# Cross-attention on one core: queries and outputs as seven block products in place of eight

## The chip, the cores and the metric

The kernel runs on one core of a Trainium2 chip. The metric is the device time of one execution in microseconds, as the median of several runs. In the profile PE is TensorE, PEld its loading of weights, DVE is VectorE, ACT is ScalarE, POOL is GpSimd, and SP is the engine whose queue issues most DMAs. All data are fp32.

## The reference, cut to what matters

Four layers of cross-attention, each followed by a feed-forward part, are added to x (4 batch elements of 256 tokens, 256 wide). The context has 4 x 512 rows of 128. Layers 1, 2 and 3 have the same attention, and the change is in them:

```python
def _L1_xattn_ref(text_hidden, vision_tokens, vision_mask, Wq, Wk, Wv, Wo):
    # N_HEADS = 16, N_KV_HEADS = 8, HEAD_DIM = 128, D_TEXT = 256, D_VISION = 128
    q = (text_hidden @ Wq).reshape(B, T_text, N_HEADS, HEAD_DIM).transpose(0, 2, 1, 3)
    k = (vision_tokens @ Wk).reshape(B, T_vis, N_KV_HEADS, HEAD_DIM).transpose(0, 2, 1, 3)
    v = (vision_tokens @ Wv).reshape(B, T_vis, N_KV_HEADS, HEAD_DIM).transpose(0, 2, 1, 3)
    k = jnp.repeat(k, GROUPS, axis=1)
    v = jnp.repeat(v, GROUPS, axis=1)
    scores = jnp.einsum('bhtd,bhsd->bhts', q, k) / scale
    ...
    attn = jax.nn.softmax(scores, axis=-1)
    out = jnp.einsum('bhts,bhsd->bhtd', attn, v)
    return out.transpose(0, 2, 1, 3).reshape(B, T_text, N_HEADS * HEAD_DIM) @ Wo
...
x = x + _L1_xattn_ref(_layernorm(x, axis=-1), ctx_1024, mask_BxS2_bf1, L1_xattn_Wq, L1_xattn_Wk, L1_xattn_Wv, L1_xattn_Wo)
x = x + _L1_ffn_ref(_layernorm(x, axis=-1), ...)
```

The feed-forward part of layer 1 routes each token to 2 of 8 experts, that of layer 2 picks one of two networks per token, and that of layer 3 works on 64 chosen tokens of each batch element.

## The kernel before

The weights are folded ahead of each of the three attention stages: `m_sb` holds Wq times Wk per head (256 x 128), `n_sb` holds Wv times Wo per head (128 x 256). With them a head's queries are 128 wide, its scores are products with the context itself (`cT`), its values are the context (`c_sb`), and its output is a product with `n_sb`.

`attention(L, ...)` runs over 32 units in order: 4 batch elements `b`, and in each of them 8 pairs of heads `hp`. One unit does, as the code is written:

- `queries` of the next unit (L1689): 4 matmuls of 256 columns into a PSUM bank `mm`, copied to `qT` by ACT (L1697).
- `heads`: 4 score matmuls of 512 columns (L1704) into banks `s`, an exponential of each on ACT (L1707), 4 value matmuls (L1710) into a bank `o`, a copy to `oT` (L1714). POOL adds two halves of the 4 exponentials (`half`, L1717).
- `summed`: DVE adds again (L1723), turns 32x32 blocks (L1725) and reduces (L1729), which gives the sums for the softmax.
- Every fourth unit, `quotients`: a matmul `pz` (L1734), on DVE a bound and a reciprocal `rz` (L1743, L1744), and for each of 4 pairs a transpose `wide` on DVE (L1747) and a product on POOL (L1751) that divides `oT`.
- At `hp == 3`, `output` of the batch element before: for both halves of its tokens, 16 matmuls of 256 columns (L1760) into a bank `mm`, added to `x_sb` by DVE (L1768).

`wide` and `turned` share a ring of two buffers, as do the two buffers of each PSUM bank name. Between the units stand the layernorm of the next batch element (statistics, tokens, transposes) and, through `after`, steps of the feed-forward part for the batch element before; in layer 3 these are the router's.

The engines PE, ACT, DVE and POOL work in program order here:

```python
with tc.manual_schedule(engines={E.PE, E.Activation, E.DVE, E.Pool}):
    attention(1, *mn, after=beside1)
```

So an instruction that waits holds back all that its engine has queued behind it. The end of a stage, after the last unit, reads:

```python
output(B - 1, 0, 0, H // 2)
quotients(B - 1, 1, last=True)
if at_end:
    at_end()
output(B - 1, 1, 0, H // 2)
for c in range(NC):
    output(B - 1, c, H // 2)
```

With `last=True` two of the four products of the quotients are on DVE. The weights of the feed-forward parts (`wgu`, `wd1`, `wd2`, `wds` in layer 1) are loaded into a pool `fwp` during attention, by SP's queue.

Of the kernel before, what the change touches and what calls it, by code (L numbers as in the profile page):

```python
# [9 lines left out]
F32 = mybir.dt.float32  # L10
# [3 lines left out]
ALU = mybir.AluOpType  # L14
# [3 lines left out]
P = 128  # L18
B, S, D = 4, 256, 256
# [816 lines left out]
def bounded_path(ctx: ExitStack, tc: tile.TileContext, t, out: bass.AP, over):  # L836
# [815 lines left out]
    fwp = ctx.enter_context(tc.tile_pool(name="fwp", bufs=1))  # L1652
# [21 lines left out]
    def attention(L, m_sb, n_sb, first_xnT=None, after=None, at_end=None):  # L1674
# [4 lines left out]

        with tc.tile_pool(name=f"att{L}", bufs=2) as ap:  # L1680
            xnTs, xns, norms, qTs, outs, sums = {}, {}, {}, {}, {}, {}
            units = [(b, hp) for b in range(B) for hp in range(H // 2)]

            def queries(b, hp):
                u = f"{L}_{b}_{hp}"
                pq = bank("mm", [P, 2, S], f"pq{u}")
                for j in range(2):
                    for d in range(ND):
                        nc.tensor.matmul(  # L1689
                            pq[:, j, :],  # L1690
                            lhsT=m_sb[:, d, 2 * hp + j, :],
                            rhs=xnTs[b][:, d, :],
                            start=(d == 0),
                            stop=(d == ND - 1),
                        )
                qTs[b, hp] = ap.tile([P, 2 * S], F32, tag="qT", name=f"qT{u}")
                nc.scalar.copy(qTs[b, hp], pq.rearrange("p j s -> p (j s)"))  # L1697

            def heads(b, hp):
                u = f"{L}_{b}_{hp}"  # L1700
                pT = ap.tile([P, NK, 2 * S], F32, tag="pT", name=f"pT{u}")
                for k in range(NK):
                    ps = bank("s", [P, 2 * S], f"ps{u}_{k}")
                    nc.tensor.matmul(  # L1704
                        ps, lhsT=cT[:, b, k * P : (k + 1) * P], rhs=qTs[b, hp], start=True, stop=True
                    )
                    nc.scalar.activation(pT[:, k, :], ps, AF.Exp, bias=mbias[:, b, k : k + 1])  # L1707
                po = bank("o", [P, 2 * S], f"po{u}")
                for k in range(NK):
                    nc.tensor.matmul(  # L1710
                        po, lhsT=c_sb[:, b, k, :], rhs=pT[:, k], start=(k == 0), stop=(k == NK - 1)
                    )
                raw = ap.tile([P, 2 * S], F32, tag="oT", name=f"oT{u}", bufs=H // 2 + 5)
                nc.scalar.copy(raw, po)  # L1714
                outs.setdefault(b, []).append(raw)
                half = ap.tile([P, 2, 2 * S], F32, tag="half", name=f"half{u}", bufs=1 if L == 1 else 2)
                nc.gpsimd.tensor_tensor(half, pT[:, 0:2], pT[:, 2:4], ALU.add)  # L1717
                return half
# [12 lines left out]
            def quotients(b, quarter, last=False):  # L1731
                u = f"{L}_{b}_{quarter}"
                pz = bank("t", [P, 4, NB], f"pz{u}")
                nc.tensor.matmul(  # L1734
                    pz.rearrange("p i f -> p (i f)"),
                    lhsT=quad,
                    rhs=sums.pop((b, quarter)).rearrange("p i f -> p (i f)"),
                    start=True,
                    stop=True,
                )  # L1740

                rz = ap.tile([P, 4, NB], F32, tag="rz", name=f"rz{u}")
                nc.vector.tensor_scalar(rz, pz, 1.0e-37, None, ALU.max)  # L1743
                nc.vector.reciprocal(rz, rz)  # L1744
                for i in range(4):
                    wide = ap.tile([P, NB, 32], F32, tag="turned", name=f"wide{u}_{i}")
                    nc.vector.transpose(wide, rz[:, i, :, None].to_broadcast([P, NB, 32]))  # L1747
                    oT = outs[b][4 * quarter + i]

                    eng = nc.vector if last and i % 2 else nc.gpsimd  # L1750
                    eng.tensor_tensor(oT, oT, wide.rearrange("p f i -> p (f i)"), ALU.mult)  # L1751

            pys = {}

            def output(b, c, h0=0, h1=H):
                if h0 == 0:
                    pys[c] = bank("mm", [P, D], f"py{L}_{b}_{c}")
                for h in range(h0, h1):
                    t0 = (h % 2) * S + c * P
                    nc.tensor.matmul(  # L1760
                        pys[c],
                        lhsT=outs[b][h // 2][:, t0 : t0 + P],
                        rhs=n_sb[:, h, :],
                        start=(h == 0),
                        stop=(h == H - 1),
                    )
                if h1 == H:
                    nc.vector.tensor_tensor(x_sb[b][:, c, :], x_sb[b][:, c, :], pys[c], ALU.add)  # L1768

            xnTs[0] = first_xnT if first_xnT is not None else layernorm(0, f"a{L}_0")[1]  # L1770
            queries(*units[0])
            for n, (b, hp) in enumerate(units):
                if b + 1 < B:
                    if hp == 2:
                        norms[b + 1] = Norm(b + 1, f"a{L}_{b + 1}")
                    elif hp == 4:
                        xns[b + 1] = norms[b + 1].tokens()
                    elif hp == 6:
                        xnTs[b + 1] = layernorm_T(xns[b + 1], f"a{L}_{b + 1}")
                if n + 1 < len(units):  # L1780
                    queries(*units[n + 1])
                half = heads(b, hp)
                if hp == 1 and b > 0:
                    quotients(b - 1, 1)
                if hp == 5:
                    quotients(b, 0)
                summed(b, hp, half)
                if hp == 3 and b > 0:
                    for c in range(NC):
                        output(b - 1, c)  # L1790
                if after:
                    after(b, hp)
            output(B - 1, 0, 0, H // 2)
            quotients(B - 1, 1, last=True)
            if at_end:
                at_end()
            output(B - 1, 1, 0, H // 2)
            for c in range(NC):
                output(B - 1, c, H // 2)
# [7 lines left out]
    FL = FE - P  # L1807
    with tc.issue_after(done["raw"]):
# [7 lines left out]
        )  # L1816
        wd1 = load_fw(
            "fb",
            [P, NE, D],
            lambda w: [(w, t["F1_wdT"][:FR, :].rearrange("(e f) n -> f e n", f=FE)[:P])],  # L1820
            "wd1",
        )
        wd2 = load_fw(
            "fc",
            [P, NE, D],
            lambda w: [(w[:FL], t["F1_wdT"][:FR, :].rearrange("(e f) n -> f e n", f=FE)[P:])],
            "wd2",
# [10 lines left out]
            "wds",  # L1838
        )
# [12 lines left out]
    f1s = ExitStack()  # L1852
    fx = f1s.enter_context(tc.tile_pool(name="f1x", bufs=1))
# [101 lines left out]
    with tc.manual_schedule(engines={E.PE, E.Activation, E.DVE, E.Pool}):  # L1955
# [4 lines left out]
        ):  # L1960

# [286 lines left out]

    with tc.issue_after(done["raw"]):
# [433 lines left out]
```

## Time and profile before

| | |
|---|---|
| median of 3 runs | 1534.7 us (1533.01 to 1537.58) |
| profiled execution | 1532.39 us, its span 1530.6 us |
| granted TensorE clock, mean | 0.988 |
| attention of layers 1, 2 and 3 | about 254 to 596, 731 to 1069 and 1146 to 1499 us of the span |
| PE busy in these three stages | 339.2 of 342.2, 335.5 of 338.5, 344.7 of 352.9 us |
| POOL busy in these three stages | 119.3, 119.4 and 119.3 us |

A row of groups has line, engine, operation, output and inputs with their shapes, the number of instructions, then the busy time in us and the mean ns of one, then the engine's idle time just before them and what ended most of it. A matmul of the code is two PE instructions. Matmuls overlap, so the mean duration of one is longer than the time from one start to the next. A row of a timeline has the start in us from the span's start, the duration, engine, line and operation; neighbouring instructions of one kind are merged.

### The profile page before, as it was taken

The numbers are of one execution on the slowest core, as the hardware profiler recorded it, in microseconds if no ns is written. First come the engines' busy times: TensorE is split into PE (matmuls) and PEld (weight loads), VectorE is DVE, ScalarE is ACT, GpSimd is POOL, SyncE is SP. The second block draws the span as 40 slices with busy tenths as digits, with TensorE's granted clock in tenths as the row PEclk, the third lists the DMA queues.
The fourth block names the chain that finished last, engine by engine and source line by source line (L and its number), as shares of the span: only waits on it lengthen the run. The fifth ranks groups of instructions, "written<-read, shape, count | busy, mean of one in ns | idle before, by whom it ended". The sixth has DMA issues, their size and how long they took to land.

```text
span 1530.6 us, 16401 instructions
## 1 busy us (share of the span) xinstructions
PE 1481.0 (97%) x6243; PEld 935.2 (61%) x6243; DVE 644.9 (42%) x1357; ACT 589.1 (38%) x1047; POOL 474.8 (31%) x354
## 2 busy tenths in 40 slices
PE   8999998999999999999999999999999999999997
PEld 7665676556565567656455656566885565565656
DVE  5666863233534435424233332425442334324363
ACT  4666332442434433234444342422234433423221
POOL 2222343243434331324244342423002343423330
PEclk9999999999999999999999999999999999999999
DMA  4000223100000003135000000000410000000000
GB/s 159 1 1 2 69 69 126 16 0 0 7 1 7 0 3 115 56 86 163 7 0 1 0 1 0 1 0 3 140 55 1 0 1 0 0 1 1 0 0 31
DMA packets 39955, 43.15 MB, mean 28 GB/s; under 512 B 3833, under 2 KB 36826, under 8 KB 39868
## 3 DMA queue, kind: packets, MB, share of 16 engines
q1 hardware_dynamic: 36892, 35.85, 7.4%
q0 software_dynamic: 1872, 5.11, 1.2%
q8 instruction: 52, 0.85, 0.2%
q10 hardware_dynamic: 1104, 1.05, 0.2%
q14 instruction: 35, 0.29, 0.1%
HBM read 36.89 MB, written 5.11 MB: 27 GB/s over the span
## 4 chain that ended last, share of the span: by engine, by line
PE 84%; DVE 9%; POOL 3%; issue 2%; ACT 1%; DMA 0%; POOLq 0%; DVEq 0%; ACTq 0%
PE ps L1704 20%; PE po L1710 20%; PE pq L1689 10%; PE py L1760 10%; PE ph L2308 2%; PE po L2345 2%; PE pgu L2130 2%; PE ps L1313 2%; PE po L1323 2%; PE pyf L1440 1%; POOL oT L1751 1%; PE pyr L2155 1%; PE paf L1390 1%; DVE wide L1747 1%; POOL yg L2169 1%
## 5 line engine op out<-in xcount | busy, mean ns | idle before, releaser
L1717 POOL TENSOR_TENSOR half<-pT 128x1024 f32<-128x1024 f32 x96 | 225.0, 2344 | 579.1 <-ACT pT L1707 406.9
L1704 PE MATMUL ps<-qT,cT 128*128 128x512 f32 x768 | 350.1, 599 | 3.8 <-ACT qT L1697 3.8
L1710 PE MATMUL po<-pT,c_sb 128*128 128x512 f32 x768 | 345.3, 592 | 0.0
L1707 ACT ACTIVATE pT<-ps,mbias 128x512 f32<-128x512 f32 x384 | 263.3, 687 | 77.9 <-PE ps L1704 68.0
L1710 PEld LDWEIGHTS po<-pT,c_sb 128*128 128x128 f32 x768 | 146.0, 190 | 183.6 <-issue 183.1
L1704 PEld LDWEIGHTS ps<-qT,cT 128*128 128x128 f32 x768 | 147.7, 193 | 149.7 <-issue 140.6
L1723 DVE TENSOR_TENSOR half<-half 128x512 f32<-128x512 f32 x96 | 75.0, 782 | 357.4 <-POOL half L1717 357.4
L1689 PE MATMUL pq<-xnT_a,m_sb 128*128 128x256 f32 x768 | 183.4, 383 | 0.7 <-ACT xnT_a L923 0.7
L1760 PE MATMUL py<-n_sb,oT 128*128 128x256 f32 x768 | 169.3, 380 | 1.3 <-POOL oT L1751 1.3
L1689 PEld LDWEIGHTS pq<-xnT_a,m_sb 128*128 128x128 f32 x768 | 143.6, 191 | 39.8 <-issue 14.1
L1760 PEld LDWEIGHTS py<-n_sb,oT 128*128 128x128 f32 x768 | 145.4, 190 | 26.1 <-issue 4.8
L1714 ACT COPY oT<-po 128x512 f32<-128x512 f32 x96 | 56.2, 585 | 263.4 <-PE po L1710 263.4
L1697 ACT COPY qT<-pq 128x512 f32<-128x512 f32 x96 | 56.1, 585 | 255.5 <-PE pq L1689 246.5
L1751 POOL TENSOR_TENSOR oT<-oT,wide 128x512 f32<-128x512 f32 x90 | 121.0, 1375 | 67.3 <-DVE wide L1747 67.3
L1317 ACT ACTIVATE pT<-ps 128x512 f32<-128x512 f32 x128 | 66.1, 603 | 40.8 <-PE ps L1313 40.6
L1747 DVE STREAM_TRANSPOSE wide<-rz 128x512 f32<-128x512 f32 x96 | 65.1, 699 | 28.8 <-POOL oT L1751 28.0
L1725 DVE STREAM_TRANSPOSE turned<-half 128x512 f32<-128x512 f32 x96 | 68.3, 711 | 4.8
L1729 DVE TENSOR_REDUCE sums<-turned 128x16 f32<-128x512 f32 x96 | 65.8, 686 | 3.3
L1743 DVE TENSOR_SCALAR rz<-pz 128x64 f32<-128x64 f32 x24 | 5.4, 224 | 137.1 <-PE pz L1734 137.1
L1768 DVE TENSOR_TENSOR x_sb<-x_sb,py 128x256 f32<-128x256 f32 x24 | 10.1, 421 | 115.9 <-PE py L1760 115.9
L2110 POOL DMA_INDIRECT xg<-xd,who x23 | 22.0, 956 | 59.3 <-PE pxg L2118 33.0
L1313 PE MATMUL ps<-qT,kT 16*128 16x256 f32 x512 | 38.6, 408 | 0.0
(343 smaller groups left out, 1511.3 us busy)
## 6 DMA issues: line engine op xcount, KB each, us to landing
wo<-in_L_wo SPq DMA_DIRECT2D x13, 512.0 KB, 7.1
wq<-in_L_wqT SPq DMA_DIRECT2D x12, 512.0 KB, 4.1
yd<-yr SPq DMA_DIRECT2D x23, 128.0 KB, 1.7
w<-in_F_w SPq DMA_DIRECT2D x2, 1024.0 KB
wgu<-in_F_wgT SPq DMA_DIRECT2D x1, 1760.0 KB, 6.9
wgu<-in_F_wuT SPq DMA_DIRECT2D x1, 1760.0 KB, 10.8
wk<-in_L_wkT SPq DMA_DIRECT2D x12, 128.0 KB, 4.2
wv<-in_L_wvT SPq DMA_DIRECT2D x12, 128.0 KB, 5.9
```

The costliest lines, as they stand in the source:

```text
L1313: nc.tensor.matmul(ps[j][:, k, :], lhsT=kTs[b][r, hg, k0 : k0 + P], rhs=qTs[b][r, hg, :], start=True, stop=True)
L1317: nc.scalar.activation(pT[kp][:, j], ps[j], AF.Exp)
L1689: nc.tensor.matmul(pq[:, j, :], lhsT=m_sb[:, d, 2 * hp + j, :], rhs=xnTs[b][:, d, :], start=(d == 0), stop=(d == ND - 1),)
L1704: nc.tensor.matmul(ps, lhsT=cT[:, b, k * P : (k + 1) * P], rhs=qTs[b, hp], start=True, stop=True)
L1707: nc.scalar.activation(pT[:, k, :], ps, AF.Exp, bias=mbias[:, b, k : k + 1])
L1710: nc.tensor.matmul(po, lhsT=c_sb[:, b, k, :], rhs=pT[:, k], start=(k == 0), stop=(k == NK - 1))
L1717: nc.gpsimd.tensor_tensor(half, pT[:, 0:2], pT[:, 2:4], ALU.add)
L1723: nc.vector.tensor_tensor(part, half[:, 0], half[:, 1], ALU.add)
L1725: nc.vector.transpose(turned.rearrange("p f i -> p (f i)"), part)
L1747: nc.vector.transpose(wide, rz[:, i, :, None].to_broadcast([P, NB, 32]))
L1751: eng.tensor_tensor(oT, oT, wide.rearrange("p f i -> p (f i)"), ALU.mult)
L1760: nc.tensor.matmul(pys[c], lhsT=outs[b][h // 2][:, t0 : t0 + P], rhs=n_sb[:, h, :], start=(h == 0), stop=(h == H - 1),)
```

## The change

Queries and outputs are products of 2x2 blocks of 128x128. They are now formed from seven block products in place of eight (Winograd's form of Strassen's scheme): sums of the blocks of both operands are made ahead, seven products go into two PSUM banks, and one ACT copy and four DVE sums combine them.

- The sums of `m_sb` (DVE, 4 operations per pair of heads) and `n_sb` (POOL, 4 per pair) are made once per stage, in the units of the first batch element; those of `xnT` (DVE, 4) once per batch element; those of the divided `oT` (POOL, 4) for each unit.
- The first two pairs of the first batch element keep the queries of before (`first_queries`).
- Outputs are formed for each four pairs instead of eight, into banks `s` instead of `mm`. The last four pairs of a stage keep the plain product (`last_output`), both halves of the tokens in one bank `s`.
- The divisions are spread over two units, two in each; the layernorm steps stand one unit earlier; the queries of the next unit are combined on DVE.
- `wgu` and `wds` of layer 1 move to another pool, `wd1` and `wd2` are loaded after the attention stage of layer 1, and `fwp` is opened after the feed-forward part of layer 1.

```diff
+            def s_sums(eng, a11, a12, a21, a22, s1, s2, s4):
+                eng.tensor_tensor(s1, a21, a22, ALU.add)
+                eng.tensor_tensor(s2, s1, a11, ALU.subtract)
+                eng.tensor_tensor(s4, a12, s2, ALU.subtract)
+                eng.tensor_tensor(a21, a11, a21, ALU.subtract)
...
+            def m_sums(hp):
+                s_sums(nc.vector, *m_blocks(hp), *(m_x[:, hp, i, :] for i in range(3)))
...
+            def n_sums(hp):
+                t_sums(nc.gpsimd, *n_blocks(hp), *n_more(hp))
...
+            def seven(of, u, tag="mm", between=None):
+                ps = []
+                for n, which in (("a", (1, 6, 7, 5)), ("b", (2, 3, 4))):
+                    if n == "b" and between:
+                        between()
+                    p = bank(tag, [P, len(which), P], f"p{n}{u}")
+                    for k, pair in enumerate(of):
+                        for at, i in enumerate(which):
+                            lhsT, rhs = pair[i]
+                            nc.tensor.matmul(
+                                p[:, at, :], lhsT=lhsT, rhs=rhs,
+                                start=(k == 0 and at == 0), stop=(k == len(of) - 1 and i == which[-1]),
+                            )
+                    ps.append(p)
+                return ps
+
+            def four(w, pa, pb):
+                nc.scalar.copy(w[:, 0, :], pa[:, 0, :])
+                nc.vector.tensor_tensor(w[:, 1, :], w[:, 0, :], pa[:, 1, :], ALU.add)
+                nc.vector.tensor_tensor(w[:, 2, :], w[:, 1, :], pa[:, 2, :], ALU.add)
+                nc.vector.tensor_tensor(w[:, 1::2, :], w[:, 1:3, :], pa[:, 3:4, :].to_broadcast([P, 2, P]), ALU.add)
+                nc.vector.tensor_tensor(w[:, 0:3, :], w[:, 0:3, :], pb, ALU.add)
+
+            def queries(b, hp):
...
+                four(qTs[b, hp], *seven([of], f"q{L}_{b}_{hp}"))
...
+            def divided(b, hp, eng):
+                wide = ap.tile([P, NB, 32], F32, tag="turned", name=f"wide{L}_{b}_{hp}")
+                nc.vector.transpose(wide, rzs[b, hp // 4][:, hp % 4, :, None].to_broadcast([P, NB, 32]))
+                eng.tensor_tensor(outs[b, hp], outs[b, hp], wide.rearrange("p f i -> p (f i)"), ALU.mult)
+
+            def o_sums(b, hp, eng):
+                ox = oxs[b, hp] = ap.tile([P, 3, P], F32, tag="ox", name=f"ox{L}_{b}_{hp}", bufs=5)
+                s_sums(eng, *o_blocks(outs[b, hp]), *(ox[:, k, :] for k in range(3)))
...
+                def products(self, between=None):
+                    self.ps = seven(self.of, f"o{self.u}", "s", between)
+
+                def add(self):
+                    w = ap.tile([P, 4, P], F32, tag="qT", name=f"w{self.u}", bufs=3)
+                    four(w, *self.ps)
+                    x = x_sb[self.b].rearrange("p c (e d) -> p (c e) d", d=P)
+                    nc.vector.tensor_tensor(x, x, w, ALU.add)
...
             for n, (b, hp) in enumerate(units):
...
+                if n == 0:
+                    first_queries(1)
+                    x_sums(0)
+                elif n + 1 < len(units):
                     queries(*units[n + 1])
-                half = heads(b, hp)
-                if hp == 1 and b > 0:
-                    quotients(b - 1, 1)
-                if hp == 5:
-                    quotients(b, 0)
+                if b == 0:
+                    m_sums((hp + 2) % (H // 2))
+                last, i = ((b, 0), hp - 4) if hp >= 4 else ((b - 1, 1), hp)
+                prev = last[0] >= 0
+                h0 = 4 * last[1]
+                if prev and i == 1:
+                    for k in (2, 3):
+                        divided(last[0], h0 + k, nc.gpsimd)
+                    o_sums(last[0], h0, nc.gpsimd)
+                elif prev and i == 2:
+                    for k in (1, 2):
+                        o_sums(last[0], h0 + k, nc.gpsimd)
+                half = heads(b, hp, (lambda: quotients(*last)) if prev and i == 0 else None)
+                if prev and i == 0:
+                    for k in (0, 1):
+                        divided(last[0], h0 + k, nc.gpsimd)
+                if prev and i == 2:
+                    o_sums(last[0], h0 + 3, nc.gpsimd)
+                if b + 1 < B and hp == 6:
+                    x_sums(b + 1)
                 summed(b, hp, half)
-                if hp == 3 and b > 0:
-                    for c in range(NC):
-                        output(b - 1, c)
+                if b == 0:
+                    n_sums(hp)
+                if prev and i == 2:
+                    out = Output(*last)
+                    if last != (B - 1, 0):
+                        out.products()
+                        out.add()
                 if after:
                     after(b, hp)
-            output(B - 1, 0, 0, H // 2)
-            quotients(B - 1, 1, last=True)
+            out.products(lambda: quotients(B - 1, 1))
+            for k in range(4):
+                divided(B - 1, 4 + k, nc.vector if k % 2 else nc.gpsimd)
+            out.add()
             if at_end:
                 at_end()
-            output(B - 1, 1, 0, H // 2)
-            for c in range(NC):
-                output(B - 1, c, H // 2)
+            last_output(B - 1)
...
+            w1d = [fp.tile([P, NE, D], F32, tag=f"wd{i}", name=f"wd{i}", bufs=1) for i in (1, 2)]
+            wd1, wd2 = w1d
+            w1r = t["F1_wdT"][:FR, :].rearrange("(e f) n -> f e n", f=FE)
+            nc.sync.dma_start(wd1, w1r[:P])
+            nc.sync.dma_start(wd2[:FL], w1r[P:])
```

In the loop `i` is a unit's place after the fourth pair of a quarter: at `i == 0` the quotients, at `i == 2` the output of that quarter.

## Prediction

> **What bounds the kernel now.** I read the page first: the engine totals and the chain that ended last.
>
> ```profile
> span 1530.6 us, 16401 instructions
> PE 1481.0 (97%) x6243; PEld 935.2 (61%) x6243; DVE 644.9 (42%) x1357; ACT 589.1 (38%) x1047; POOL 474.8 (31%) x354
> ...
> PE 84%; DVE 9%; POOL 3%; issue 2%; ACT 1%; DMA 0%; POOLq 0%; DVEq 0%; ACTq 0%
> ```
>
> TensorE (PE) is busy nearly all the time and carries 84% of the chain, so a matmul that goes away is worth its own time, as long as nothing else comes late. Next the groups of instructions, for the two matmul groups that the change rewrites and the two GpSimd (POOL) groups that are there already:
>
> ```profile
> L1717 POOL TENSOR_TENSOR half<-pT 128x1024 f32<-128x1024 f32 x96 | 225.0, 2344 | 579.1 <-ACT pT L1707 406.9
> L1723 DVE TENSOR_TENSOR half<-half 128x512 f32<-128x512 f32 x96 | 75.0, 782 | 357.4 <-POOL half L1717 357.4
> L1689 PE MATMUL pq<-xnT_a,m_sb 128*128 128x256 f32 x768 | 183.4, 383 | 0.7 <-ACT xnT_a L923 0.7
> L1760 PE MATMUL py<-n_sb,oT 128*128 128x256 f32 x768 | 169.3, 380 | 1.3 <-POOL oT L1751 1.3
> L1352 POOL TENSOR_TENSOR oT<-o 128x256 f32<-128x256 f32 x16 | 11.8, 739 | 68.5 <-DVE o L1351 64.4 <-PE py L1358 3.7 <-DVE nrf L1406 0.4
> ```
>
> POOL sits idle 579 us ahead of L1717: it has room on the average. The 383 ns of a matmul overlap with the next one, so I take its pitch from the timeline of PE, where one row starts when the row before has been streamed in; columns are start and duration in us.
>
> ```profile
> 505.58 1.89 PE L1689 MATMUL pq<-xnT_a,m_sb 128*128 128x256 f32 x8
> 507.31 3.60 PE L1704 MATMUL ps<-qT,cT 128*128 128x512 f32 x8
> 510.74 1.45 PE L1710 MATMUL po<-pT,c_sb 128*128 128x512 f32 x3
> ...
> 703.65 1.06 PE L968 MATMUL pm<-wk,wq 128*128 128x128 f32 x8
> 704.54 1.02 PE L989 MATMUL pn<-wo,wv 128*128 128x512 f32 x2
> ```
>
> Eight instructions of 256 columns take 507.31 - 505.58 = 1.73 us (216 ns each), eight of 512 take 3.43 us, eight of 128 take 0.89 us (112 ns). Each matmul of the code is two instructions here. A head pair costs 1.73 + 3.43 + 3.43 = 8.59 us of PE, plus 1.73 for its outputs. Last the timeline of VectorE (DVE) and POOL where they meet:
>
> ```profile
> 480.21 4.18 POOL L1751 TENSOR_TENSOR oT<-oT,wide 128x512 f32<-128x512 f32 x3
> 482.15 1.11 DVE L1723 TENSOR_TENSOR half<-half 128x512 f32<-128x512 f32 x1
> 484.35 2.34 POOL L1717 TENSOR_TENSOR half<-pT 128x1024 f32<-128x1024 f32 x1
> 484.71 2.46 DVE L908 TENSOR_SCALAR xn_f<-x_sb,mv_f,rstd_f 128x256 f32<-128x256 f32 x2
> 487.09 0.68 DVE L1723 TENSOR_TENSOR half<-half 128x512 f32<-128x512 f32 x1
> ```
>
> The same addition takes 0.68 us alone and 1.11 us beside POOL, three POOL products take 4.18 us where 3 x 1.27 = 3.81 is usual, and two DVE operations of 0.41 us take 2.46 when they come while POOL runs. They take turns.
>
> **TensorE.** Seven block products of 128 columns are 14 instructions: 14 x 0.112 = 1.57 us in place of 8 x 0.216 = 1.73, so 0.16 us per pair and use. Queries: 30 of 32 pairs in each of 3 layers, 90 x 0.16 = 14.4. Outputs: 28 of 32, 84 x 0.16 = 13.4. Together -27.8 us. Bounds: 107 ns (half of 216) would give -40; the mean of 25.9 us over the 192 instructions of L968, 135 ns, would give +28. Here weights change with every product as in L968, whose undisturbed pitch is 112; I take that.
>
> **New work that stays hidden.** Combining the seven products is one ACT copy (about 0.27, from L1697's 585 ns at 512 columns and 373 at 256) and four DVE sums of 128, 128, 256 and 384 columns, 0.29 + 0.29 + 0.42 + 0.56 = 1.55 us by the rows of DVE between 128 and 512 columns. A pair has some 8.4 us before its scores need them: nothing, as long as DVE is not more than some 5 us late; then each late microsecond counts. In the first batch element DVE also has four sums of m per pair, 4 x 0.29. The loads of wd1 and wd2 (1.4 MB) leave the time of attention for its end in layer 1, ahead of the xd write and of the next layer's weights on SP's queue; 1.76 MB landed within 6.9 and 10.8 us, and the first expert block is gathered 28 us and reads wd1 41 us after that end: 0, and up to 10 if that cover were gone.
>
> **New work that does not stay hidden.** The sums of heads are four POOL operations of 128x128 per pair, which no row shows. L1352 has 727 ns at 256 columns (median), L1751 1.27 us at 512, L1717 2.34 at 1024: 2.1 ns per column and 0.19 fixed, so 0.456 us. Bounds: 0.27 (columns alone) and 0.73 (the 256 row itself). Two of four wait for the one before (0.05 us each): 1.9 us a pair.
>
> I walk one output through the queues; time 0 is when PE ends the scores of the pair whose slot holds the quotients. POOL's half is 1.0 to 3.35 (exp, then 2.34). DVE's addition waits for POOL's next product, ends 5.1; transpose and reduction 6.6; layernorm's statistics, which stand next, 7.9; the four sums of the next pair's queries 9.6; the third quotient's transpose 10.3. Only now can POOL divide heads 3 and 4: 12.85; sums of pair 1: 14.7; half of the next pair (ready at 9.5) 17.0; sums of pairs 2 and 3 with DVE's addition between, 21.1; half of the third pair 23.5; sums of pair 4: 25.4. PE in the meantime: three pairs at 8.43 us with their small matmuls reach the output's products at 21.1 and the fourth pair's products, 3 x 0.90 later, at 23.8. So PE waits 1.6 us, in front of all that it has queued. For the first output of a layer POOL also has four sums of n per pair and DVE those of m: 3.3. For the seventh, without a next layernorm: 0.8. 3 x (3.3 + 5 x 1.6 + 0.8) = +36 us. Each 0.1 us on the POOL operation moves the 16 of them in the chain, 1.6 us per output, 33 us in all.
>
> [...]
>
> **The end of each layer.** The last output takes the score bank of the output before it, and that is free only when three of the combining sums have read it, which DVE has queued behind the four quotients:
>
> ```profile
> 585.24 0.22 DVE L1743 TENSOR_SCALAR rz<-pz 128x64 f32<-128x64 f32 x1
> ...
> 588.67 1.29 DVE L1747 STREAM_TRANSPOSE wide<-rz 128x512 f32<-128x512 f32 x2
> 590.00 1.33 DVE L1751 TENSOR_TENSOR oT<-oT,wide 128x512 f32<-128x512 f32 x1
> 590.84 5.45 PE L1760 MATMUL py<-n_sb,oT 128*128 128x256 f32 x24 [0.59 <-POOL oT L1751]
> ```
>
> From the start of rz to the last product is 591.33 - 585.24 = 6.1 us; with 1.0 for the three sums and 0.4 to 0.9 from pz to rz, the bank is free 7.6 to 8.1 us after pz, and PE has 0.17 + 2.69 us of products until then, 0.94 more in layer 3. It idles about 4.7, 5.2 and 3.7, 13.6 in all, where it idles 2.2 today (L1760's last 48 at 10.37 take 11.58, 11.39, 10.42): +11.4. Both halves of x now come at the very end: the next norm is some 1 us later, which layer 1 (0.2 us of slack before its transposes) and layer 3 feel: +1.8. The last pair of a layer finds its queries' sums late by 1.0: +3.
>
> **What goes the other way.** PE waits 13.8 us in the attention stages today for layernorm and router steps (1.25 us at 571.4, 2 to 3 us three times in layer 3). POOL no longer does four quotients in one slot before them, and the output waits give DVE time. Bounds 0 and -13.8; I take -6.
>
> **Sum.** -27.8 + 36 + 11.4 + 1.8 + 3 - 6 = +18.4. The profiled execution is 1532.39 (span 1530.6 and 1.8 around it), 2.3 under the median of the three runs; on it 1550.8, on the median of 1534.7: 1553.
>
> **Rivals.** Late sums on POOL (the forecast): for it, the chain above; 0.55. *POOL keeps up*: if a 128x128 operation costs 0.36 or less, or the port is free more often than in the walk, the ordinary waits vanish and the first output's falls to 1.5: -27.8 + 4.5 + 11.4 + 1.8 + 3 - 6 = -13, 1522, faster; for it POOL's 31%, against it the three sizes that lie on one line; it decides at 1.6 us less in the chain. 0.22. *POOL slower*: 0.55 us an operation, from issue or port waits that the long rows hide: +1.5 x 21 = +32, 1585; 0.15. *No gain on TensorE*: the products cost 124 ns, as a mix of 112 and L968's mean of 135; the 28 us are gone, 1581; 0.08.
>
> The range leaves out most of the second case and the top of the third and fourth: 1526 to 1585. A change of under 0.3% (4.6 us) can't be told from none; between 1530.1 and 1539.3 lie the forecast's low flank and part of the second case, 0.12; faster 0.22; slower 0.66.
>
> **What would show it.** In the profile after: the block products at 112 ns start to start; POOL's 128x128 additions at 0.45 to 0.46 us; PE idle of 1 to 2 us ahead of the fourth pair's output products, released by POOL; 4 to 5 us ahead of the last output, released by DVE. No wait on POOL there, or block products at 125 ns or more, would make it wrong.

## The result, and the profile after

The changed kernel takes 1543.5 us (median of 6 runs, 1539.5 to 1545.8) against 1535.0 for the kernel before in the same comparison: a ratio of 1.0054, interval 1.0035 to 1.0073. That is 8.5 us slower. The prediction had 18.4 us slower (1553): the right direction, but more than twice the measured size. The profiled execution is 1542.4 us with a span of 1540.6, so 10.0 us longer in its span than the one of before. I account for those 10.0 us, not for the 8.5.

First the page of the changed kernel, engine totals and the chain that ended last:

```profile
PE 1468.4 (95%) x7287; PEld 955.3 (62%) x7287; DVE 885.8 (57%) x1948; ACT 564.7 (37%) x1068; POOL 683.5 (44%) x786
...
PE 57%; POOL 22%; DVE 15%; issue 3%; ACT 1%; DMA 0%; POOLq 0%; DVEq 0%; ACTq 0%
```

PE was 97% busy and carried 84% of the chain before. Now POOL carries 22% of it although it is busy only 44% of the time. The groups of PE say where the two meet; the last columns are PE's idle time ahead of the group and what ended it:

```profile
L1771 PE MATMUL pao<-n_x,ox 128*128 128x128 f32 x336 | 67.9, 284 | 17.9 <-POOL ox L1697 17.9
L1771 PE MATMUL pao<-n_sb,oT 128*128 128x128 f32 x264 | 52.7, 282 | 5.9 <-POOL oT L1699 5.9
```

Both are the output's block products, and both wait on sums of heads. With a third such group (`n_t,oT`, 3.7 us) PE idles 27.5 us there. Counted from start to start, as in the account below, the same waits are 34.1 us, since the modelled duration of a matmul reaches into the wait behind it. Now the timeline of PE, for the pitch and for one such wait (start, duration):

```profile
505.22 0.39 PE L1771 MATMUL paq<-xnT_a,m_sb 128*128 128x128 f32 x2
505.45 0.39 PE L1771 MATMUL paq<-xx,m_x 128*128 128x128 f32 x2
...
454.80 0.39 PE L1771 MATMUL pao<-n_sb,oT 128*128 128x128 f32 x2
456.34 0.49 PE L1771 MATMUL pao<-n_x,ox 128*128 128x128 f32 x2 [1.15 <-POOL ox L1697]
457.28 0.49 PE L1771 MATMUL pao<-n_t,oT 128*128 128x128 f32 x2 [0.46 <-POOL oT L1699]
...
457.99 0.64 PE L1771 MATMUL pbo<-n_sb,oT 128*128 128x128 f32 x2
458.42 0.63 PE L1771 MATMUL pbo<-n_sb,ox 128*128 128x128 f32 x2
```

Two instructions start every 0.22 us, 112 ns each, as forecast. Ahead of the fourth pair PE waits twice, 1.9 us in all over the pitch. Behind that wait two instructions take 0.43 us: half the rate. The timeline of DVE and POOL shows where the wait begins, 15 us earlier:

```profile
439.40 0.17 DVE L902 TENSOR_SCALAR ve_a<-mv_a 128x2 f32<-128x2 f32 x1
439.48 0.28 DVE L1781 TENSOR_TENSOR qT<-qT,paq 128x128 f32<-128x128 f32 x1
...
440.64 0.56 DVE L1784 TENSOR_TENSOR qT<-qT,pbq 128x384 f32<-128x384 f32 x1
441.12 1.30 DVE L1849 STREAM_TRANSPOSE wide<-rz 128x512 f32<-128x512 f32 x2
...
436.15 1.73 POOL L1850 TENSOR_TENSOR oT<-oT,wide 128x512 f32<-128x512 f32 x1
441.90 2.49 POOL L1850 TENSOR_TENSOR oT<-oT,wide 128x512 f32<-128x512 f32 x2 [1.55 <-DVE wide L1849]
444.35 0.46 POOL L1696 TENSOR_TENSOR ox<-oT 128x128 f32<-128x128 f32 x1
...
452.66 2.35 POOL L1816 TENSOR_TENSOR half<-pT 128x1024 f32<-128x1024 f32 x1
454.97 0.45 POOL L1696 TENSOR_TENSOR ox<-oT 128x128 f32<-128x128 f32 x1
```

POOL has ended two divisions at 437.9 and, but for one 0.7 us operation, stands until 441.9. The transposes it needs are behind the four sums of the next queries on DVE. From then on it is never idle until the fourth pair's sums at 454.97, and those stand behind a `half` of 2.35 us. This is the walk of the prediction, link by link.

**An account of the three attention stages.** From the starts of all PE rows I take the time to the next start, and subtract the pitch: 112 ns at 128 columns, 216 at 256, 429 at 512, 110 for the small products. An excess over 60 ns counts as *half clock* where the time to the next start is at most 15% over twice the pitch, and as *wait* where it is longer. "Rest" is the total less both. The last two columns are stretches outside attention: up to the first query product of layer 1, and between the attention of layers 1 and 2. Layer 2 begins here with its first query product (723.5 us in the kernel before); the 731 us ahead of the prediction are where its scores begin. All in us, from one profile each; E1 to E12 are the experiments below.

| kernel | total | waits | half clock | rest | up to layer 1 | layers 1 to 2 |
|---|---|---|---|---|---|---|
| before | 1040.5 | 20.8 | 7.9 | 1011.9 | 253.9 | 127.4 |
| before again (E6) | 1037.5 | 20.6 | 5.2 | 1011.7 | 253.8 | 133.2 |
| after | 1042.2 | 46.4 | 12.8 | 983.0 | 257.8 | 131.0 |
| after again (E5) | 1040.8 | 45.7 | 12.2 | 982.9 | 256.0 | 131.5 |
| E1, output a unit later | 1053.0 | 48.6 | 21.4 | 983.1 | 264.2 | 127.4 |
| E2, last sums ahead of half | 1000.4 | 13.0 | 4.3 | 983.0 | 258.7 | 125.7 |
| E3, queries alone | 1014.5 | 12.4 | 5.1 | 996.9 | 258.7 | 124.0 |
| E4, outputs alone | 1012.9 | 10.2 | 5.0 | 997.7 | 253.9 | 127.4 |
| E7, one addition more | 1107.6 | 88.8 | 35.3 | 983.5 | 260.6 | 129.9 |
| E8, layernorm earlier | 1038.5 | 23.2 | 3.6 | 1011.8 | 258.6 | 129.9 |
| E9, divisions spread | 1021.9 | 6.8 | 3.8 | 1011.3 | 264.2 | 127.5 |
| E10, divisions ahead of queries | 1009.7 | 18.6 | 8.3 | 982.8 | 260.6 | 129.7 |
| E11, E2 and E10 | 992.3 | 6.3 | 3.2 | 982.8 | 256.8 | 131.0 |
| E12, last output's bank | 1058.8 | 58.3 | 16.4 | 984.1 | 255.8 | 130.1 |

The rest depends on the products alone: 1011.3 to 1011.9 with eight, 982.8 to 983.5 with seven in both places (E12 has a few small products more), about 997 with seven in one. The attention as a whole became only 1.7 us longer: 28.9 us of products saved, 25.6 of waits and 4.9 of half clock added. The name of that column is borne out by the clock that the profile grants to TensorE: in the changed kernel it is 1.00 from 454 to 456 us and 0.50 from 457.9 to 459.9, behind the wait shown above. But short waits of the same size fall into the column too: 8.3 of its 12.8 us lie at a granted clock of 0.50, and 5.4 of the 7.9 before.

### The profile page after: what moved, and what is told of

Same layout as the page of the kernel before. It is cut to its first block, busy times and chain, and to the rows that moved or that the text cites. A ratio compares the mean times of both kernels' runs of the same rounds, so it can differ in the third digit from the quotient of the medians.

```text
span 1540.6 us, 19664 instructions
## 1 busy us (share of the span) xinstructions
PE 1468.4 (95%) x7287; PEld 955.3 (62%) x7287; DVE 885.8 (57%) x1948; ACT 564.7 (37%) x1068; POOL 683.5 (44%) x786
## 4 chain that ended last, share of the span: by engine, by line
PE 57%; POOL 22%; DVE 15%; issue 3%; ACT 1%; DMA 0%; POOLq 0%; DVEq 0%; ACTq 0%
PE ps L1801 13%; POOL half L1816 8%; PE po L1809 8%; PE pbo L1771 4%; PE paq L1771 3%; POOL oT L1850 3%; POOL ox L1697 3%; DVE half L1822 2%; PE pbq L1771 2%; POOL ox L1698 2%; POOL oT L1699 2%; POOL ox L1696 2%; PE ph L2454 2%; PE po L2491 2%; PE pgu L2275 2%
## 5 line engine op out<-in xcount | busy, mean ns | idle before, releaser
L1822 DVE TENSOR_TENSOR half<-half 128x512 f32<-128x512 f32 x96 | 100.3, 1044 | 297.8 <-POOL half L1816 297.8
L1771 PE MATMUL pao<-n_x,ox 128*128 128x128 f32 x336 | 67.9, 284 | 17.9 <-POOL ox L1697 17.9
L1771 PEld LDWEIGHTS paq<-xnT_a,m_sb 128*128 128x128 f32 x360 | 59.0, 191 | 27.4 <-PE po L1809 13.6
L1771 PE MATMUL paq<-xnT_a,m_sb 128*128 128x128 f32 x360 | 70.0, 276 | 0.0
L1771 PE MATMUL paq<-xx,m_x 128*128 128x128 f32 x360 | 69.6, 275 | 0.0
L1771 PEld LDWEIGHTS pao<-n_x,ox 128*128 128x128 f32 x336 | 51.8, 195 | 20.8 <-POOL ox L1697 20.7
L1771 PE MATMUL pao<-n_sb,oT 128*128 128x128 f32 x264 | 52.7, 282 | 5.9 <-POOL oT L1699 5.9
L1784 DVE TENSOR_TENSOR qT<-qT,pbq 128x384 f32<-128x384 f32 x90 | 49.9, 554 | 9.7 <-DVE qT L1783 0.5
L1771 PEld LDWEIGHTS paq<-xx,m_x 128*128 128x128 f32 x360 | 54.7, 192 | 0.0
L1780 ACT COPY qT<-paq 128x128 f32<-128x128 f32 x90 | 23.8, 265 | 80.2 <-PE paq L1771 80.2
```

The source lines that it names most:

```text
L1771: nc.tensor.matmul(p[:, at, :], lhsT=lhsT, rhs=rhs, start=(k == 0 and at == 0), stop=(k == len(of) - 1 and i == which[-1]),)
L1822: nc.vector.tensor_tensor(part, half[:, 0], half[:, 1], ALU.add)
```

## The experiments

The theory after this reading: the loss is the wait on POOL's sums of heads, a chain of DVE's order and POOL's order, and it can be taken away by order alone. Ratios are to the kernel before in the same comparison.

**E1, the output one unit later.**

```diff
-                if prev and i == 2:
+                if prev and i == 3:
                     out = Output(*last)
```

> The output of a quarter is formed one unit later (i == 3 in place of i == 2); all else as in the changed kernel. Theory 1 (the loss is TensorE's wait on GpSimd's sums of heads, 34 us of waits and 9 us of half clock behind them in the 18 outputs inside the loop): with 8.4 us more for the sums these waits vanish, 1543.5 - 43.5 = 1500 us, 1496 to 1508, and no start-to-start time above 0.3 us is left among the output products. Rival 2 (GpSimd and VectorE are behind as a whole, and the wait only moves to the scores, which need the combined queries, or to the next output): at most half of it is gained, 1520 to 1532. Rival 3 (nine buffers of oT are too few once eight pairs are held): the value products wait for the copy, 1535 or more.

Measured: 1551.9 us, 1.0108 (1.0086 to 1.0130), slower than the changed kernel. The output's products start without any wait now, but the queries of the next batch element wait instead, by the groups of PE of E1:

```profile
L1771 PE MATMUL paq<-xnT_a,m_sb 128*128 128x128 f32 x360 | 73.6, 287 | 9.7 <-DVE xnT_a L1705 7.7 <-DVE qT L1783 1.8
L1771 PE MATMUL paq<-xx,m_x 128*128 128x128 f32 x360 | 73.0, 286 | 15.1 <-DVE xx L1703 15.1
```

Their sums of `xnT` stand on DVE behind an addition that waits 6.2 us for a `half`, which POOL makes late, behind divisions and sums of heads; the first of them then takes 1.71 us beside POOL's next `half`, where 0.28 is usual. Both are the same in the changed kernel (6.2 and 1.71 us); there PE has the output's products and their wait ahead of these queries, which gives DVE the time. So the mechanism of rival 2 held, but not its bound of 1520 to 1532: all of the wait came back, and more. The time lies where rival 3 put it, but no value product waits in E1, so its mechanism is out. The late thing was POOL's and DVE's whole order, not this one product. The waits of the router steps in layer 3 came back too (9.3 us ahead of `pw`).

**E2, the fourth pair's sums ahead of `half`.**

```diff
-                    for k in (1, 2):
+                    for k in (1, 2, 3):
                         o_sums(last[0], h0 + k, nc.gpsimd)
...
-                if prev and i == 2:
-                    o_sums(last[0], h0 + 3, nc.gpsimd)
```

> The fourth pair's sums of heads stand ahead of the third unit's half (2.34 us) in GpSimd's order; outputs stay where they are. Theory 1: the chain to the fourth pair's products is 2.3 us shorter, the 15 ordinary waits of 1.9 us go, and the first output of each layer waits about 1.5 in place of 3.5: 15 x 1.9 + 3 x 2 = 34 us less, 1505 to 1515. Rival 2: half comes 1.9 us later and with it VectorE's addition and the sums that combine the next queries; where VectorE has no room the scores wait for them, and the time stays at 1530 to 1545.

Measured: 1496.0 us, 0.9744 (0.9725 to 0.9762), 9 us under the expectation's lower end. Of the outputs inside the loop only the first of each layer waits, 0.9 us. The gain over the changed kernel, 47.5 us, is larger than the 31.5 by which the waits on POOL fall. Other things went with them: half clock falls from 12.8 to 4.3 us, and the wait ahead of `pw` from 3.4 to 1.6; 4.4 us of the two profiles' difference lie outside attention.

**E3 and E4, one half of the change alone.** E3 leaves out the sums of heads and of `n_sb` and forms each quarter's output by plain products in a bank `s`; E4 leaves out the sums of `m_sb` and `xnT` and copies plain queries by ACT.

```diff
 E3
-                    out = Output(*last)
+                    out = Plain(*last)      # 16 matmuls of 256 columns, as last_output
 E4
-                    queries(*units[n + 1])
+                    first_queries(units[n + 1][1], units[n + 1][0])
```

> Queries alone as seven block products; outputs are plain products of four pairs in a bank s, without sums of n or of heads. Theory 1: against the kernel before -15.8 us of products, about -11 of layernorm, router and half-clock waits: 1508 to 1514. By the prediction's own terms (-14.4, +3, +1.8, -6): 1519. Rival: VectorE's four sums for m and four for combining, in front of what the half and the quotients need, cost as much as they bring: 1528 to 1538.

> Outputs alone as seven block products; queries are the plain products copied by ScalarE for every pair, without sums of m and x and without combining on VectorE. Theory 1 with VectorE as a link (the combining of the next queries, 1.6 us, stands ahead of the third quotient's transpose): the 15 ordinary waits fall from 1.9 us to some 0.3, 1535 - 15.6 + 43.5 - 15 x 1.6 - 3 x 2 - 11 = 1522 us, 1518 to 1532. If VectorE's combining is no link, the waits stay: 1550 to 1556. If the block products of outputs bring nothing in themselves, 1540 or more with the waits gone.

Measured: E3 1508.0 us, 0.9838 (0.9802 to 0.9874); E4 1505.9, 0.9815 (0.9797 to 0.9833). Either half alone is a gain, of 26 and 28 us in this comparison, and both together are a loss. Half the products are saved each time (rest 996.9 and 997.7). In E4 POOL has the same sums of heads as in the changed kernel and PE waits for them 3.2 us in place of 34: without the queries' sums on DVE ahead of them, POOL's divisions are not late. E4 came out 16 us under the 1522 of its expectation: of the 13.5 us of waits and half clock that the sum had left to the outputs, only those 3.2 us are there, most of them at the first output of each layer.

**E5 and E6, both kernels once more.** No edit.

> The changed kernel once more, for a second profile. Theory A (the 3.8 us before the attention of layer 1 and the 3.6 us between layers 1 and 2, in code that the change leaves alone, are spells of half clock that come and go between executions): the time is again 1543.5 within 2, but the profile's stretch before the first query product is not 257.8 and that between layers 1 and 2 not 131.0; five other profiles had 253.9 to 264.2 and 124.0 to 127.4. Theory B (the program settles them, by the longer code or the moved loads): 257.8 and 131.0 again, within 0.3.

> The kernel before once more, for a second profile, as a yardstick for the same question. Theory A: the stretch before the first query product differs from 253.9 by a spell or two (2 to 6 us), and its attention stages agree with 342.2, 346.0 and 352.3 within 1. Theory B: 253.9 and 127.4 again.

Measured: 1543.2 us, 1.0060 (1.0035 to 1.0084), and 1537.9, 1.0005 (0.9990 to 1.0020). The attention stages repeat (table). The stretch between layers 1 and 2 was 127.4 and 133.2 us in the same kernel before, so the 3.6 us there can't be laid at the change. The stretch up to layer 1 repeated in the kernel before (253.9, 253.8), differed by 1.8 us in the changed one, and spread over 253.9 to 264.2 in the others; E8 and E9, which have the code of the kernel before there, had 258.6 and 264.2. Its differences are spells in which the starts are twice as far apart: the granted clock of the first 50 us is 0.93 in the kernel before and 0.80 in E9. Between layers 1 and 2 there is also a wait ahead of the products that fold layer 2's weights, of 2.5 us in the changed kernel, but of 2.4 and 1.9 in E6 and E8 too. Neither theory holds in full: whether the changed kernel has on the average a spell more outside the attention stays open.

**E7, one addition more per pair on POOL.**

```diff
             def o_sums(b, hp, eng):
...
-                s_sums(eng, *o_blocks(outs[b, hp]), *(ox[:, k, :] for k in range(3)))
+                blocks = o_blocks(outs[b, hp])
+                eng.tensor_tensor(ox[:, 0, :], blocks[2], blocks[3], ALU.add)
+                s_sums(eng, *blocks, *(ox[:, k, :] for k in range(3)))
```

> The changed kernel with the first of the four sums of heads made twice on GpSimd for every pair (same result): 4 x 0.46 = 1.84 us more in the chain of each output. By the prediction's slope all of it is waited for, 18 outputs x 1.84 = 33 us and some 3 us of half clock behind it: 1575 to 1585, the waits ahead of the output products rising from 34 to about 67 us. Rival: GpSimd waits for VectorE's turns inside the chain and takes the addition into that idle time: under 15 us, 1545 to 1558.

Measured: 1608.2 us, 1.0466 (1.0440 to 1.0493), 65 us over the changed kernel, where 31 to 41 were expected. The group of PE in E7:

```profile
L1771 PE MATMUL pao<-n_x,ox 128*128 128x128 f32 x336 | 73.6, 304 | 53.3 <-POOL ox L1697 53.3
```

The waits rose by 42 us and not 33: in the timeline of POOL the added operation takes 0.53 us to the start of the next one, not its 0.46, which makes 18 x 4 x 0.53 = 38 of the 42. And the half clock rose by 23 us where I had put 3. The rival (idle time of POOL takes it in) is out.

**E8 and E9, parts of the change on the kernel before.** E8 moves the layernorm steps one unit earlier; E9 does that and spreads the divisions over two units, as the change has it.

```diff
 E8 and E9
-                    if hp == 2:
+                    if hp == 1:
                         norms[b + 1] = Norm(b + 1, f"a{L}_{b + 1}")
... (4 becomes 3, 6 becomes 5)
 E9
+                if prev and i == 1:
+                    for k in (2, 3):
+                        divided(last[0], 4 * last[1] + k, nc.gpsimd)
+                half = heads(b, hp, (lambda: quotients(*last)) if prev and i == 0 else None)
+                if prev and i == 0:
+                    for k in (0, 1):
+                        divided(last[0], 4 * last[1] + k, nc.gpsimd)
```

> The kernel before with one part of the change alone: the layernorm steps of the next batch element stand one unit earlier (hp 1, 3, 5 in place of 2, 4, 6). If the nine waits of 0.5 us between pz and the layernorm's transposes go, -4.4 us: 1530. If the quotients or the outputs, which stand in units 1, 3 and 5, take the time back, the waits of 0.5 us move to other products and the time stays at 1533 to 1537.

> The kernel before with two parts of the change alone: the divisions spread over two units (two on GpSimd in each, quotients between scores and values) and the layernorm steps one unit earlier; no block products. In the traces of the changed kernel the waits for layernorm and router steps are 11 us fewer (14.6 to 3.7). If the spread divisions did that: 1536 - 10 = 1526, 1522 to 1529, and no wait between pz and the layernorm's transposes. If it is the block products (which lengthen TensorE's units by their waits and give VectorE time), the time stays at 1533 to 1538, as with the layernorm alone (1537.5).

Measured: E8 1537.5 us, 1.0009 (0.9993 to 1.0025), no change; E9 1520.4, 0.9892 (0.9869 to 0.9915), a gain of 14 us without any block product, 2 us under the lower end of the expectation. The groups of PE for the router's product and for a transpose of the feed-forward norm, of the kernel before and then of E9:

```profile
L2443 PE MATMUL pw<-diag,ones 128*128 128x128 f32 x16 | 3.2, 331 | 7.3 <-DVE diag L2436 7.3
L1887 PE MATMUL pxn_f<-ident,xn_f 128*128 128x128 f32 x16 | 2.6, 286 | 1.4 <-DVE xn_f L908 1.3
```

```profile
L2450 PE MATMUL pw<-diag,ones 128*128 128x128 f32 x16 | 2.5, 279 | 0.8 <-DVE diag L2443 0.8
L1894 PE MATMUL pxn_f<-ident,xn_f 128*128 128x128 f32 x16 | 2.4, 273 | 0.0
```

In E8 the nine waits of 0.5 us behind `pz` went, but those ahead of `pxn_f` and `pw` grew from 9.5 to 16.3 us: they moved. In E9 0.5 us of them is left (ahead of the gather's product `pxg`). So the norm and router steps were late because of the four divisions in one slot, or of the quotients' place: E9 spreads the divisions and also puts the quotients between scores and values, and the two were not tried apart. This part of the change was a gain on its own that the forecast counted at 6 us, and the gains of E3 and E4 contain it.

**E10, the divisions ahead of the next queries.** In program order DVE's two transposes stand before the sums of the queries.

```diff
+                if prev and i == 1:
+                    for k in (2, 3):
+                        divided(last[0], h0 + k, nc.gpsimd)
                 if n == 0:
                     first_queries(1)
...
                 if prev and i == 1:
-                    for k in (2, 3):
-                        divided(last[0], h0 + k, nc.gpsimd)
                     o_sums(last[0], h0, nc.gpsimd)
```

> The changed kernel with the second two divisions ahead of the next queries in program order: on VectorE their two transposes then stand before the four sums that combine the queries, not behind them (1.65 us from first sum to first transpose in the trace). If that is a link of the chain, GpSimd's divisions start 1.6 us earlier, the 15 ordinary waits fall from 1.9 to 0.3 and the first of each layer by 1.6: 18 x 1.6 + some 4 us of half clock = 33 us, 1505 to 1515. Rival: GpSimd or the ring of two buffers wide/turned holds the transposes, or the later combining makes the scores wait: 1530 to 1543.

Measured: 1509.6 us, 0.9815 (0.9788 to 0.9842), where 1505 to 1515 was expected. The timeline of DVE and POOL at the same place of E10:

```profile
435.63 0.67 DVE L1849 STREAM_TRANSPOSE wide<-rz 128x512 f32<-128x512 f32 x1
436.23 0.25 DVE L1781 TENSOR_TENSOR qT<-qT,paq 128x128 f32<-128x128 f32 x1
...
435.84 2.50 POOL L1850 TENSOR_TENSOR oT<-oT,wide 128x512 f32<-128x512 f32 x2
```

The transposes come first, POOL follows its 0.7 us operation (ended 435.88) at once, and the ordinary waits fall from 1.9 to 0.5 us or less: the link that the walk names, at the size that it gives.

**E11, both orders.**

> Both edits: the divisions ahead of the next queries, and the fourth pair's sums ahead of the third unit's half. With the half's edit alone 1496 us were left with 0.9 us of waits at the first output of each layer and 1.0 at the last pair's scores. If all waits ahead of the output products are gone already, only those of the first outputs can go: 1493 to 1496, not to be told from 1496. Rival: VectorE is late by 1.6 us for the combined queries, and the last pair's scores or the norms pay: 1497 to 1505.

Measured: 1490.9 us, 0.9701 (0.9677 to 0.9725), the fastest of all and 5 us under E2, a little below the expectation. No output product waits within the layers, and the last pair's scores wait only in layer 3 (1.3 us). E9's 1520.4 less the 28.5 us of products between the two (1011.3 to 982.8) is 1491.9: no other cost of the change is to be seen. The page of E11:

```profile
PE 1449.5 (97%) x7287; PEld 942.6 (63%) x7287; DVE 883.0 (59%) x1948; ACT 565.2 (38%) x1068; POOL 679.1 (46%) x786
...
PE 89%; DVE 7%; POOL 2%; issue 1%; ACT 1%; another core or an unknown queue 0%; DMA 0%; POOLq 0%; ACTq 0%; DVEq 0%
```

POOL is as busy as in the changed kernel (44% there) and has 2% of the chain in place of 22%.

**E12, the last output in the bank that is still being read.** Two banks are held around it.

```diff
+                held = [bank("s", [P, NC, D], f"held{L}_{k}") for k in range(2)]
+                for k in range(2):
+                    nc.tensor.matmul(held[k][:, 0, :NB], lhsT=quad, rhs=ident[:, :NB], start=True, stop=True)
                 py = bank("s", [P, NC, D], f"py{L}")
... (and the same two matmuls once more behind py)
```

> The changed kernel with two further score banks held by two small matmuls before and after the last output of each layer, so that this output gets the bank that VectorE's combining sums still read, as the prediction had it. By the prediction's term: 13.6 us of waits at the three ends in place of the 1.2 of the trace, +12.4; by the changed kernel's own trace the third combining sum ends 4.0, 4.0 and 3.6 us after the last output's start, +11.6. With some half clock behind waits of 4 us (0 to 2 us each): 1543.5 + 12 to 18 = 1555 to 1562, and 4 to 5 us of idle released by VectorE ahead of the last output. Rival: the bank was not what kept the end short, for the products behind it would wait for VectorE's divisions anyway: 1543 to 1548.

Measured: 1563.0 us, 1.0176 (1.0151 to 1.0201), 1 us over the expectation. The group of PE of E12:

```profile
L1889 PE MATMUL py<-n_sb,oT 128*128 128x256 f32 x96 | 26.1, 440 | 11.5 <-DVE w L1783 11.5
```

PE idles 11.5 us at the three ends, released by the third combining sum, and half clock rises by 3.6 us. From start to start the waits are 4.9, 4.2 and 3.6 us, where the prediction had 4.7, 5.2 and 3.7. So the wait that the prediction put at the end of each layer does exist, at nearly its price, in a kernel where the last output gets that bank; the changed kernel is not such a one.

## Why the prediction was right in sign and wrong in size

Its terms, in order, against the profile after less the profile before (us):

| step | forecast | measured |
|---|---|---|
| products saved | -27.8 | -28.9 |
| PE waits on the sums of heads | +36 | +34.1 |
| end of each layer | +11.4 | -0.5 |
| later norm | +1.8 | +0.9 (stretch after layer 3, 31.7 to 32.6; none seen in layer 1) |
| last pair's queries | +3 | +3.1 |
| fewer layernorm and router waits | -6 | -11.0 |
| half clock behind waits | not in the sum | +4.9 (2.9 of it at a granted clock of 0.50) |
| code outside attention | not in the sum | +7.4 (257.8 and 131.0 against 253.9 and 127.4) |

**The step that failed is the end of each layer.** It says that the last output takes the score bank of the output before it. That rests on two buffers for each bank name, as the description of the kernel ahead of the prediction has it, and that is wrong: the line of `bank` (L855) gives `s` four buffers, `mm` two and only the others one. The two halves of the output before hold two of them, and the last output gets a third. The timeline of PE and DVE at the end of layer 1 shows it:

```profile
596.71 0.39 PE L1771 MATMUL pbo<-n_x,oT 128*128 128x128 f32 x2
597.68 7.17 PE L1886 MATMUL py<-n_sb,oT 128*128 128x256 f32 x32 [0.58 <-POOL oT L1850]
...
601.24 0.42 DVE L1783 TENSOR_TENSOR w<-w,pao 128x256 f32<-128x256 f32 x1
```

The last output starts 4.0 us before the third combining sum ends, as soon as POOL has divided the first pair. The sign that the forecast named for this term, 4 to 5 us ahead of the last output, is missing: PE waits 0.7 and 0.4 us there in layers 1 and 2, and not at all in layer 3. E12 builds the case that I had read and gets 11.5 us of idle for it. Without this term the same sum is +7.0, 1541.7 on the median of 1534.7. That this comes so near to the 1543.5 measured is luck in part, since the errors of the other terms, from -5.0 to +7.4, nearly cancel.

**The first output of a layer, the ordinary ones and the one without a norm.** Forecast waits 3.3, 1.6 and 0.8 us; measured 3.6 to 4.0, 1.4 to 1.9 and 0.3 to 0.6. That the totals agree, 36 and 34.1, is partly luck. The forecast counted seven waiting outputs a layer, five of them ordinary; the trace has six, four of them ordinary, since the seventh is formed behind the last unit and does not wait. At the forecast's own prices that makes 3 x (3.3 + 4 x 1.6 + 0.8) = 31.5, and the single waits were somewhat longer. The steps under them stand: an addition of 128x128 on POOL takes 0.455 us (0.456 forecast), the four of a pair 1.89 us from start to start (1.9; 0.53 to the next where that reads the result of the one before, 0.41 where it does not), and 2.2 where DVE's addition takes a turn. E4 and E10 show that DVE's sums for the queries are a link, E2 that `half` is one.

**The two terms beside it.** The norm and router waits were set too low, by 5 us within the stated bounds of 0 and -13.8: E9 shows that the spread of the divisions, with the order that goes with it, takes nearly all of them. Half clock was left out, and it is the price of a wait beyond the wait. These two cancel, which is luck. The 7.4 us outside the attention are of the size that one kernel's profiles differ by (E5, E6), and stay open.

**The rivals.** POOL did not keep up, though E2 and E11 turn the forecast of that case (1522) into less than 1500 by order alone; POOL was not slower than 0.46; the products cost 112 ns, not 124. The loads of `wd1` and `wd2`, put at 0, show no cost: with them moved, E3 and E4 have 124.0 and 127.4 us between the layers, and the two profiles of the kernel before 127.4 and 133.2.

**DVE and POOL at the same time.** The walk adds nothing for the combining sums beside a busy POOL, and the trace after agrees. L1783, which reads one operand from a PSUM bank, takes 0.42 us beside a POOL addition that covers it and 0.42 alone. Nor is POOL held up: its 39 additions of heads that overlap nothing on DVE but combining sums take 0.455 us, as alone. Other operations do take longer side by side: L1822, which reads no PSUM bank, 0.93 beside POOL (median) and 0.69 alone, and L1697 on POOL 0.79 beside L1822 and 0.455 alone. What sets these apart from the combining sums was not tried. Two of the rivals name a port: no run shows one, only the durations above and those in the prediction's rows.

## What to carry to other kernels

On a kernel that is bound by TensorE, work added to other engines is priced by its place in their order, not by their busy share: 0.46 us operations on an engine that is 44% busy cost 34 us in one order (the changed kernel) and nothing in another (E11). Walk the queue from the value that is needed back to the last idle time of the engine that makes it; the instructions on that walk are the ones to move. E10 moved the one that ended the idle time (34 us gained), E2 another one nearer the end (47.5 us); E1 moved the product that waits instead, and lost 8 us. Before a wait for a buffer is put into a sum, read how many buffers there are.

## What the runs showed of the hardware that I had not expected

- A wait of TensorE cost more than itself. In E7 all 14 waits of 3.2 to 3.4 us ahead of output products were followed by 10 to 25 block-product instructions at about 213 ns in place of 112; of the 6 waits of 3.0 us in the two profiles of the changed kernel 5 were, and of its 18 waits of 1.2 to 1.3 us at ordinary outputs (one or two parts) one. Behind such a wait the profile's granted clock is 0.50: from 375.8 to 380.0 us in E7, where the wait ends at 375.8. So the 42 us of waits that E7 added brought 23 us of half clock with them.
- No single length of wait decided whether slow instructions followed. The waits above are all of 3.4 us or less, and two of 2.1 to 2.2 us in E7 were followed by 13 and 19 slow instructions. One of 2.8 us in E7 was not (granted clock 1.00 from 1417 to 1420 us), nor was one of 3.7 us ahead of layer 2's first scores in the changed kernel (1.00 from 742.9 to 746.5 us).
- The granted clock repeats this as a mean over the whole execution: 0.982 in the changed kernel, 0.961 in E7, 0.987 in E11.
